# A graph layer with a mixture of experts: x multiplied before its norm, and the last experts' weights loaded elsewhere

## The chip, the cores and the metric

The kernel runs on one core of one Trainium2 chip. Its time is the device time of that core in microseconds, the median over several runs. TensorE is called PE below, VectorE DVE, ScalarE ACT, GpSimd POOL and SyncE SP; a DMA is issued from the instruction queue of SP, ACT or POOL.

## The reference

There are 3125 nodes with 256 features each, and 100000 edges sorted by their target. A layer norm of x (no gain or bias) feeds two branches: a graph convolution with a maximum over the edges of a target, and an attention-like mixer over all nodes. Their sum and x go through a second layer norm and a mixture of eight experts of which each node uses two:

```
xn = layernorm(x)
e = relu((xn[dst] - xn[src]) @ theta.T + theta_b + xn[src] @ phi.T + phi_b)
gnn = segment_max(e, dst)                   # 0 for a node with no edge
q, k, v = split(xn @ w_qkv.T)               # 8 heads of 64
dots = instance_norm(k).T @ instance_norm(v)
mix = (q @ dots / N) @ w_out.T + b_out
x = x + gnn + mix
xt = layernorm(x)
two experts by softmax(xt @ Wr + br), weights made to sum to 1
y_e = gelu(layernorm_e(xt) @ W1[e]) @ W2[e]  # 256 -> 1024 -> 256
x = x + sum of the two weighted y_e
```

## The kernel before

**Layout.** The nodes lie in 25 tiles of 128. `xnT(i)` holds the normalised tile i transposed (in the buffers `xn_lo` and `xn_hi`), `x_sb` the tile itself. The convolution is rewritten: since theta acts on the target and on the source, an edge's value is the target's `xn @ theta` plus the source's `b = xn @ (phi - theta)`, and the maximum has to be taken of the sources' `b` alone.

**Start.** While x loads, `search` (L258 to L287) finds the runs of edges in which nodes end, and POOL gathers 25 columns of keys (`run_keys`). `norm_stages` (L223), five steps skewed against each other over the tiles by `skewed`, takes mean and variance of a tile on DVE, the root on ACT, the reciprocal and `normalize` on DVE, transposes the normalised tile on PE into PSUM tile `tr`, copies it to `xnT`, multiplies by `wb = phi - theta` into PSUM tile `bp`, and copies that to `bt`. Every five tiles are stored to `b_d` in DRAM by one DMA on SP (L245 is the copy, `move` at L100 the store).

**Gathers and folds.** The edges lie in 782 steps of 128 edges, one per partition. POOL gathers the `b` rows of a step's sources (L107, 755 such gathers in the main loop), eight steps to a window in one of five buffers `wide` (named `g`), DVE folds each step into the running segment maximum (L366), and SP stores the windows to `s_d`. The steps are cut into four groups (`STEPS` = 240, 195, 194, 126), each of which finishes the nodes of its tiles (`GROUPS`: tiles 12 to 24, 5 to 11, 1 to 4, and 0).

**Behind a group.** When a group is folded, `group` (L1128) fetches the nodes' last rows from `s_d` (r gathers, POOL), `token_tile` (L422) adds the mixer's part (`without_edges`, L398, which multiplies `xnT` by theta and by the mixer's product into one PSUM tile `am` and adds x through an identity), norms the tile, and computes the router; `dispatch` (L1108) gives the rows to experts and scatters them to `xs_d` (L114). `Stream.go` (L720) is the experts' FFN of groups 0 to 2 on PE (L615 first product `hp`, L639 second product `yp`, L753 its bias), weights loaded expert by expert into three buffers `wts`. The mixer (`mixer`, L1008) runs beside the gathers of the first group.

**The last group.** Tile 0 has no scatter: `dense_tile` (L786) runs all eight experts over it in the order `DENSE` = 5, 6, 7, 0, 1, 2, 3, 4. The weights of 5, 6 and 7 are still in `wts`. Expert 0's first half is loaded into `xn_lo` during group 2's FFN, its second half into `xn_hi` when that FFN ends (L776, ACT queue); expert 1's two halves go into two `wide` buffers during the combines (L1323 to L1329, SP queue); 2, 3 and 4 (2 MB each) are loaded by `next_dense` (L1199, ACT queue) into `wts` as the first three experts are done. `scaled(k)` (L802) makes the input `xe` of phase k on DVE. Meanwhile `finale` gathers the FFN's rows `ys_d` back for every other tile (`combine`, 48 gathers), adds them (L1308) and stores them to `out` on SP. A combine chunk is four tiles, sometimes fewer, in a `wide` buffer: seven chunks follow one another.

**What sets the order.** The instruction order of PE, DVE, ACT and SP is written by the program itself. Tasks are Python generators; `start` puts one in a list and `tick` (L1063 to L1080) advances, after each gather of the main loop, every task that is due. What a task yields is the number of gather times (1.25 us) until it is due again. So a larger yield ahead of some instructions puts them later in their engines' queues, behind whatever other tasks emit meanwhile. POOL's own order is the order in which gathers and scatters are made. A transpose that stands early in PE's queue holds up everything behind it until its input is there; the maxima over nodes with no edge in tile 0 (`first_maxima`, L1207, transposes L1235) are such a place.

## Time and profile before

| what | us |
|---|---|
| median of 3 runs | 1219.15 (1218.51 to 1221.02) |
| profiled execution | 1217.85 |
| its span | 1216.0 |
| first gather of b_d rows | 48.19 |
| last gather of b_d rows | 1114.62 |
| last fold | 1120.05 |
| first matmul of the dense tile | 1140.36 |
| last store (`out<-o`) issued | 1208.98 |

All times inside the execution count from the start of its span. Busy time is what an engine spent in instructions; an instruction that waits for a semaphore shows as idle time before it, with the releaser in brackets, `[6.73 <-DMA b_d<-bt]` being 6.73 us idle, ended by a DMA. Where the releaser is called "issue", the profile shows no wait. By stretches: between 48 and 500 POOL is busy for 343.4 us and PE for 275.9 of 452; between 500 and 940 PE for 417.4 of 440; between 940 and 1006 PE for 24.1 of 66; between 1006 and 1120 PE for 106.3 of 114, with the DMA engines moving 357 GB/s; between 1120 and 1140.4 they move 97 GB/s; and in the last 75.6 us PE is busy for 61.4.

### The profile page before, as it was taken

To read this page: it belongs to the slowest core of one execution; us is meant where nothing else is said; L and a number is where in the kernel's file an instruction comes from. 1 tells how busy PE (TensorE), PEld (TensorE's weight loads), DVE (VectorE), ACT (ScalarE), POOL (GpSimd) and SP (SyncE) were. 2 spreads that over 40 slices of the span, in tenths; PEclk is the share of its full clock that TensorE was granted. 3 is DMA by queue.
4 is the path that set the end of the run, shared out by engine and by line. 5 is a ranking of instruction groups with operands and counts; after the bars stand their busy time and mean duration, and the time that the engine had idled before them with its cause. 6 is when DMAs were issued, how large, how long until landed. Compare 5 with 4: busy or idle time off the path is not lost.

```text
span 1216.0 us, 13364 instructions
## 1 busy us (share of the span) xinstructions
PE 938.2 (77%) x3929; PEld 670.4 (55%) x3929; DVE 678.6 (56%) x1998; ACT 326.0 (27%) x762; POOL 885.8 (73%) x911
## 2 busy tenths in 40 slices
PE   6556866645923548689999999979999527999986
PEld 5323433323311323258888887868887315777786
DVE  7669866685336772433333587455546764433633
ACT  4212222210101222133333343323332112332331
POOL 6677777777777777777777777777777777776733
PEclk9778888866965557889999999989999557999998
DMA  8668877666685664467888787689999658998683
GB/s 280 214 200 277 302 253 242 227 227 207 207 292 194 239 235 157 156 238 258 285 307 310 251 284 271 227 308 356 380 370 367 219 191 305 375 387 301 201 338 94
DMA packets 103928, 320.13 MB, mean 263 GB/s; under 512 B 20897, under 2 KB 44186, under 8 KB 92325
## 3 DMA queue, kind: packets, MB, share of 16 engines
q0 software_dynamic: 44032, 119.73, 31.5%
q1 hardware_dynamic: 29724, 115.08, 24.4%
q10 hardware_dynamic: 30089, 84.36, 19.3%
q8 instruction: 33, 0.54, 0.2%
q14 instruction: 50, 0.41, 0.1%
HBM read 192.05 MB, written 127.04 MB: 262 GB/s over the span
## 4 chain that ended last, share of the span: by engine, by line
PE 43%; DMA 5%; issue 4%; POOL 3%; DVE 2%; ACT 1%; ACTq 0%; POOLq 0%; DVEq 0%; SPq 0%
PE yp L639 18%; PE hp L615 18%; PE yp L753 3%; POOL g L107 2%; DMA w<-in_w 2%; DMA g<-b_d,srcI 2%; PE trf L698 1%; POOL xs_d L114 1%; DMA xn_lo<-b_d 1%; PE am L445 1%; DVE g L366 1%; PE mm L491 0%; DMA xn_hi<-xs_d 0%; DMA r<-s_d,end_i 0%; PE mm L403 0%
## 5 line engine op out<-in xcount | busy, mean ns | idle before, releaser
L107 POOL DMA_INDIRECT g<-b_d,srcI x755 | 738.2, 978 | 238.4 <-issue 203.8
L366 DVE SCALAR_TENSOR_TENSOR g<-g,cut 128x256 f32<-128x256 f32 x751 | 363.5, 484 | 356.8 <-DMA g<-b_d,srcI 339.0
L639 PE MATMUL yp<-w,hT 128*128 128x256 f32 (+1 forms) x1120 | 296.8, 387 | 0.0
L615 PE MATMUL hp<-xe,w 128*128 128x256 f32 (+2 forms) x1216 | 285.9, 361 | 11.5 <-issue 5.6
L615 PEld LDWEIGHTS hp<-xe,w 128*128 128x128 f32 x1216 | 216.7, 196 | 49.2 <-issue 18.0
L617 ACT ACTIVATE hT<-hp,sm 128x256 f32<-128x256 f32 (+2 forms) x320 | 140.2, 439 | 335.8 <-PE hp L615 335.3
L639 PEld LDWEIGHTS yp<-w,hT 128*128 128x128 f32 (+1 forms) x1120 | 201.1, 185 | 39.7 <-issue 12.4
L1012 PE MATMUL kv<-wkv,xn_lo 128*128 128x512 f32 x96 | 54.5, 720 | 38.0 <-DVE kn L1030 24.1
L1012 PE MATMUL kv<-wkv,xn_hi 128*128 128x512 f32 x104 | 59.3, 724 | 30.9 <-DVE kn L1030 30.2
L107 POOL DMA_INDIRECT g<-ys_d,from_i x48 | 46.1, 960 | 32.4 <-DVE g L1308 18.7
L445 PE MATMUL am<-cr,oh 128*128 128x257 f32 x86 | 37.3, 560 | 27.8 <-DVE r L450 19.9
L1012 PEld LDWEIGHTS kv<-wkv,xn_lo 128*128 128x128 f32 x96 | 21.1, 231 | 63.8 <-issue 60.3
L1012 PEld LDWEIGHTS kv<-wkv,xn_hi 128*128 128x128 f32 x104 | 22.8, 230 | 58.3 <-issue 55.6
L1228 DVE SCALAR_TENSOR_TENSOR xn_lo<-xn_lo,no_edge 128x256 f32<-128x256 f32 x96 | 45.9, 479 | 16.1 <-DMA xn_lo<-b_d 16.1
L401 PE MATMUL mm<-bias,ones 1*128 1x512 f32 x50 | 32.4, 731 | 16.2 <-ACT x_sb L408 12.9
L753 PE MATMUL yp<-b_sb,ident 8*128 8x256 f32 (+1 forms) x128 | 43.9, 422 | 0.0
L1016 ACT ACTIVATE sq<-kv 128x1024 f32<-128x1024 f32 x25 | 25.5, 1019 | 59.3 <-PE kv L1012 59.3
L445 PEld LDWEIGHTS am<-cr,oh 128*128 128x128 f32 x86 | 20.3, 267 | 37.1 <-issue 24.9
L709 ACT ACTIVATE xe<-trf,sm 128x256 f32<-128x256 f32 (+1 forms) x64 | 31.3, 544 | 27.6 <-PE trf L698 27.6
L1035 PEld LDWEIGHTS dots_p<-kn,vn 128*128 128x128 f32 x200 | 26.9, 199 | 19.0 <-issue 19.0
L1024 ACT ACTIVATE rsk<-var,eps 128x16 f32<-128x16 f32 x25 | 7.7, 308 | 110.7 <-DVE var L1021 110.7
L698 PE MATMUL trf<-ident,xn_hi 128*128 128x128 f32 (+1 forms) x128 | 19.2, 275 | 22.2 <-DMA xn_hi<-xs_d 22.2
(285 smaller groups left out, 991.1 us busy)
## 6 DMA issues: line engine op xcount, KB each, us to landing
s_d<-g SPq DMA_DIRECT2D x80, 1024.0 KB
w<-in_w ACTq DMA_DIRECT2D x84, 512.0 KB
w<-in_w ACTq DMA_DIRECT2D x6, 2048.0 KB
g<-b_d,srcI POOLq DMA_INDIRECT x755, 4.5
s_d<-g SPq DMA_DIRECT2D x13, 896.0 KB
xn_hi<-xs_d ACTq DMA_DIRECT2D x12, 512.0 KB
xs_d<-zero ACTq DMA_DIRECT2D x8, 512.0 KB
b_d<-bt SPq DMA_DIRECT2D x5, 640.0 KB
```

The costliest lines, as they stand in the source:

```text
L107: got = nc.gpsimd.indirect_dma_start(out=to, out_offset=None, in_=table, in_offset=row_index(index))
L366: nc.vector.scalar_tensor_tensor(g[:, j, :], last, cut[:, t:t + 1], g[:, j, :], op0=OP.add, op1=OP.max)
L401: nc.tensor.matmul(am, ones[0:1, :], bias, start=True, stop=False)
L445: nc.tensor.matmul(r2, picks[k], carried[g], start=(k == 0), stop=(k == len(slices) - 1))
L615: nc.tensor.matmul(hp[:, 0:n], w1t[:, c, f, :], xe[:, c, 0:n], start=(c == 0), stop=(c == 1))
L617: nc.scalar.activation(hT[f][:, 0:n], hp[:, 0:n], AF.Gelu, bias=sm[:, 4 + f, e:e + 1])
L639: nc.tensor.matmul(yp[r][0:part, :], hT[q][:, r * part:(r + 1) * part], w2t[:, q, :], start=(q == 0), stop=(q == FC - 1 and self.whole))
L698: nc.tensor.transpose(tr[:, c, r * n:(r + 1) * n], self.held["xs", u // 2][0:n, u % 2 * 2 + r, c * P:(c + 1) * P], ident[0:n, 0:n])
L709: nc.scalar.activation(xe[:, c, 0:n], self.held["tr", u][:, c, 0:n], AF.Identity, bias=sm[:, 2 + c, e:e + 1], scale=sm[:, c, e:e + 1])
L753: nc.tensor.matmul(yp[0:n, :], ident[0:E, e:e + 1].to_broadcast([E, n]), b2_sb, start=False, stop=True)
L1012: nc.tensor.matmul(kv[:, k, :], xnT(i, c), wkv[:, c, k * INNER:(k + 1) * INNER], start=(c == 0), stop=(c == 1))
L1228: nc.vector.scalar_tensor_tensor(of_k[:, k, :], b, no_edge[:, k, i:i + 1], of_k[:, k, :], op0=OP.add, op1=OP.max)
```

## The change

Five things are done.

1. The first norm is no longer applied to x before the transposes. x itself is transposed (`of_x`) and multiplied (`of_sources`); the weights (`wb`, theta in `am_w`, the mixer's `wkv` and `wq`) are centred over their input dimension (`centred`: a matmul with ones and one DVE operation), so that the mean of x drops out, and the products are scaled by the tile's reciprocal deviation `rs_x` when they leave PSUM. Deviations are taken for five tiles at a time (`deviations`). The transposes run `lead` = 7 tiles ahead of the products; the stores to `b_d` are cut by `STORES`, the last of them having two tiles. The keys' gathers are started before `wb` is made. `without_edges` brings the bias and x in through a diagonal of the deviations.
2. Steps around the first lot of group 2's FFN are put closer together (`soon`).
3. Expert 1's two halves and expert 0's second half are loaded by `more_weights`, started after the last fold, on SP's queue, each into a buffer that a one-column memset claims first. The dense tile's first input is made when the FFN's last lot begins ("last lot").
4. The scatters of groups 0 and 1 come five gathers later (yield 14 in place of 9).
5. A yield of 8 stands before the transposes of `first_maxima`.

Parts of the diff that only rename or allocate, and the variant for other graphs at the end of the file, are left out.

```diff
--- before.py
+++ after.py
@@ -48,6 +48,7 @@
 REST = T - COL[G]
+STORES = (0, 5, 10, 15, 20, 23, NT)
 W = 8
@@ -220,31 +223,43 @@
-    def norm_stages(work, ps, i, wb=None, b_rows=None, held=None):
-
-        mean, var = moments(work, x_sb[:, i, :], 0)
-        rs = work.tile([P, 1], F32, name="rs")
-        nc.scalar.activation(rs, var, AF.Sqrt, bias=eps)
-        yield
-        nc.vector.reciprocal(rs, rs)
-        xn = work.tile([P, D], F32, name="xn")
-        normalize(xn, x_sb[:, i, :], mean, rs)
+    def of_x(work, ps, i):
+
+        st = work.tile([P, nc.vector.BN_STATS_DIM], F32, name="st0")
+        nc.vector.bn_stats(st, x_sb[:, i, :])
+        mv = work.tile([P, nc.vector.BN_AGGR_DIM], F32, name="mv0")
+        nc.vector.bn_aggr(mv, st)
+        nc.vector.tensor_copy(std[:, i:i + 1], mv[:, 1:2])
         tr = ps.tile([P, 2, P], F32, name="tr")
         for c in range(2):
-            nc.tensor.transpose(tr[:, c, :], xn[:, c * P:(c + 1) * P], ident)
+            nc.tensor.transpose(tr[:, c, :], x_sb[:, i, c * P:(c + 1) * P], ident)
         yield
         nc.scalar.copy(xnT(i), tr)
+
+    def deviations(i0, i1):
+        nc.scalar.activation(std[:, i0:i1], std[:, i0:i1], AF.Sqrt, bias=eps)
         yield
-        if wb is not None:
-            bp = ps.tile([P, D], F32, name="bp")
-            for c in range(2):
-                nc.tensor.matmul(bp, xnT(i, c), wb[:, c, :], start=(c == 0), stop=(c == 1))
-            yield
-            if i % 5 == 0:
-                held["bt"] = work.tile([P, 5, D], F32, name="bt", bufs=2)
-            nc.scalar.copy(held["bt"][:, i % 5, :], bp)
-            if i % 5 == 4:
-                move(nc.sync, b_rows[:, i - 4:i + 1, :], held["bt"])
+        nc.vector.reciprocal(rs_x[:, i0:i1], std[:, i0:i1])
+
+    def of_sources(work, ps, i, wb, b_rows, held):
+
+        bp = ps.tile([P, D], F32, name="bp")
+        for c in range(2):
+            nc.tensor.matmul(bp, xnT(i, c), wb[:, c, :], start=(c == 0), stop=(c == 1))
+        yield
+        i0 = max(k for k in STORES if k <= i)
+        if i == i0:
+            held["bt"] = work.tile([P, 5, D], F32, name="bt", bufs=2)
+        nc.scalar.activation(held["bt"][:, i - i0, :], bp, AF.Copy, scale=rs_x[:, i:i + 1])
+        if i + 1 in STORES:
+            move(nc.sync, b_rows[:, i0:i + 1, :], held["bt"][:, 0:i + 1 - i0, :])
+
+    def centred(w, p):
+
+        for c in range(2):
+            nc.tensor.matmul(p, ones, w[:, c, :], start=(c == 0), stop=(c == 1))
+        nc.vector.scalar_tensor_tensor(w, p[:, None, :].to_broadcast([P, 2, p.shape[-1]]), -1.0 / D, w, op0=OP.mult,
+                                       op1=OP.add)
@@ -395,17 +410,20 @@
+    diag = keep.tile([P, 2, P], F32, name="diag")
+
     def without_edges(ps, i):
+        nc.scalar.activation(diag[:, i % 2, :], ident, AF.Copy, scale=std[:, i:i + 1])
         am = ps.tile([P, 2 * D], F32, name="mm")
-        nc.tensor.matmul(am, ones[0:1, :], bias, start=True, stop=False)
+        nc.tensor.matmul(am, diag[:, i % 2, :], bias, start=True, stop=False)
         for c in range(2):
             nc.tensor.matmul(am, xnT(i, c), am_w[:, c, :], start=False, stop=False)
-        nc.tensor.matmul(am[:, D:2 * D], ident, x_sb[:, i, :], start=False, stop=True)
+        nc.tensor.matmul(am[:, D:2 * D], diag[:, i % 2, :], x_sb[:, i, :], start=False, stop=True)
         on_pe(3.1)
         yield 3
-        nc.scalar.copy(xn2(i), am[:, 0:D])
-        nc.scalar.copy(x_sb[:, i, :], am[:, D:2 * D])
+        for to, k in ((xn2(i), 0), (x_sb[:, i, :], 1)):
+            nc.scalar.activation(to, am[:, k * D:(k + 1) * D], AF.Copy, scale=rs_x[:, i:i + 1])
@@ -736,12 +754,13 @@
                 if ("xe", u) not in self.held:
+                    soon = self.lots[u][0] == G - 2
                     self.rows(u // 2)
-                    yield 8
+                    yield 3 if soon else 8
                     self.turn(u)
-                    yield 2
+                    yield 1 if soon else 2
                     self.scaled(u)
-                    yield 2
+                    yield 1 if soon else 2
                 g, e, h = self.lots[u]
@@ -768,12 +787,13 @@
                 w1t, w2t = self.held["w", q]
+                if u + 1 == len(self.lots) and not self.open:
+                    clock["last lot"] = True
                 for _ in units.run(e, w1t, self.held["xe", u], w2t, done, between, 2, self.half(u)):
...
                 dense_w[DENSE[k]] = self.held["w", q - 2 + k]
-            dense_half(0, 1, xn_hi[:, 0:FC, :].rearrange("p i d -> p (i d)"), nc.scalar)
             clock["through"] = True
@@ -802,9 +821,13 @@
+        if ready is not None:
+            while "last lot" not in ready:
+                yield 1
+        scaled(0)
+        yield 1
         while ready is not None and "through" not in ready:
             yield 1
-        scaled(0)
         o = act.tile([P, D], F32, name="o", bufs=1)
@@ -862,18 +885,45 @@
     move(nc.scalar, wb, phiT.rearrange("(c p) o -> p c o", p=P))
+    am_b = once.tile([1, 3 * D], F32, name="am_b")
+    move(nc.scalar, am_b[:, 0:D], bout)
+    move(nc.scalar, am_b[:, D:3 * D], gbias)
     run, keys, run_keys = search(ea, once, ps0, dst)
     load_x()
+    run_keys()
     nc.vector.tensor_sub(wb, wb, am_w[:, :, 0:D])
...
-    run_keys()
     b_rows = b_d.rearrange("(i p) d -> p i d", p=P)
     b_held = {}
-    skewed((norm_stages(work, ps1, i, wb, b_rows, b_held) for i in range(NT)), ((4, 5), (3, 4), (2, 3), (1, 2), (0, 0)))
+    tiles = [of_x(work, ps1, i) for i in range(NT)]
+    by_five = [deviations(i, i + 5) for i in range(0, NT, 5)]
+    sources = [of_sources(work, ps1, i, wb, b_rows, b_held) for i in range(NT)]
+    lead = 7
+    for k in range(NT + lead + 1):
+        if 0 <= k - lead - 1:
+            next(sources[k - lead - 1], None)
+        if 0 <= k - 1 < NT:
+            next(tiles[k - 1], None)
+        if k < NT:
+            next(tiles[k], None)
+        for ago in (1, 0):
+            if 0 <= k - ago < NT and (k - ago) % 5 == 4:
+                next(by_five[(k - ago) // 5], None)
+        if k == 2:
+            centred(wb, ps1.tile([P, D], F32, name="bp"))
+        if 0 <= k - lead < NT:
+            next(sources[k - lead], None)
+    nc.vector.tensor_add(am_b[:, D:2 * D], am_b[:, D:2 * D], am_b[:, 2 * D:3 * D])
+    bias_p = ps1.tile([P, 2 * D], F32, name="tr")
+    for k in range(2):
+        nc.tensor.matmul(bias_p[:, k * D:(k + 1) * D], ones[0:1, :], am_b[:, (1 - k) * D:(2 - k) * D],
+                         start=True, stop=True)
+    centred(am_w[:, :, 0:D], ps1.tile([P, D], F32, name="bp"))
+    nc.scalar.copy(bias, bias_p)
     first.close()
@@ -902,11 +950,14 @@
         yield 20
-        nc.vector.tensor_add(bias[:, 0:D], am_b[:, D:2 * D], am_b[:, 2 * D:3 * D])
-        nc.vector.tensor_copy(bias[:, D:2 * D], am_b[:, 0:D])
         move(nc.scalar, wq_sb, wq.rearrange("(r p) d -> p r d", p=P))
         move(nc.scalar, wo_sb, woT.rearrange("(r p) o -> p r o", p=P))
-        yield 10
+        yield 8
+        for r in range(4):
+            nc.vector.tensor_reduce(wq_m[:, r:r + 1], wq_sb[:, r, :], AX.X, OP.add)
+        nc.vector.tensor_scalar(wq_m, wq_m, 1.0 / D, None, op0=OP.mult)
+        yield 2
+        nc.vector.tensor_tensor(wq_sb, wq_sb, wq_m[:, :, None].to_broadcast([P, 4, D]), OP.subtract)
         move(nc.scalar, s_d[0:1, :], low)
@@ -1004,6 +1055,9 @@
         nc.vector.tensor_tensor(wkv_h, wkv_h, wm[:, :, None].to_broadcast([P, 4 * HEADS, DH]), OP.subtract)
+        kv = p2.tile([P, 2, INNER], F32, name="kv")
+        for k in range(2):
+            centred(wkv[:, :, k * INNER:(k + 1) * INNER], kv[:, k, :])
@@ -1013,9 +1067,10 @@
         sq = mixp.tile([P, 2 * HEADS, DH], F32, name="sq")
-        nc.scalar.activation(sq, kv.rearrange("p k (h e) -> p (k h) e", e=DH), AF.Square)
+        nc.scalar.activation(sq, kv.rearrange("p k (h e) -> p (k h) e", e=DH), AF.Square,
+                             scale=rs_x[:, i:i + 1])
         vn = mixp.tile([P, INNER], F32, name="vn")
-        nc.scalar.copy(vn, kv[:, 1, :])
+        nc.scalar.activation(vn, kv[:, 1, :], AF.Copy, scale=rs_x[:, i:i + 1])
         yield 3
@@ -1025,7 +1080,8 @@
         both = mixp.tile([P, HEADS], F32, name="both")
-        nc.vector.tensor_mul(both, rs[:, 0:HEADS], rs[:, HEADS:2 * HEADS])
+        nc.vector.scalar_tensor_tensor(both, rs[:, 0:HEADS], rs_x[:, i:i + 1], rs[:, HEADS:2 * HEADS], op0=OP.mult,
+                                       op1=OP.mult)
         kn = mixp.tile([P, HEADS, DH], F32, name="kn")
@@ -1117,7 +1173,7 @@
         yield from slots(ro, mm, g, half, i0, i1, made[0], taken)
-        yield 1 if g == G - 2 else 9
+        yield 1 if g == G - 2 else 14
         put = []
@@ -1229,6 +1285,7 @@
         most = at_hand["first"].tile([P, 2, FIRST], F32, name="most")
+        yield 8
         for c in range(2):
@@ -1320,13 +1377,6 @@
             yield 2 * nt
-            if g == 0 and i == i0 + W // 2:
-
-                while "shared" not in clock:
-                    yield 1
-                yield 6
-                for k in range(2):
-                    dense_half(1, k, wide.tile([P, HALF], F32, name="g"))
         if i1 == NT:
@@ -1337,6 +1387,19 @@
             yield from combines(g)
+
+    def more_weights():
+
+
+        for k in range(2):
+            to = wide.tile([P, HALF], F32, name="g")
+            nc.vector.memset(to[:, 0:1], 0.0)
+            dense_half(1, k, to)
+        while "last lot" not in clock:
+            yield 1
+        to = xn_hi[:, 0:FC, :].rearrange("p i d -> p (i d)")
+        nc.vector.memset(to[:, 0:1], 0.0)
+        dense_half(0, 1, to)
@@ -1362,6 +1425,8 @@
             clock["last"] = last
+            if g == G - 1:
+                start(more_weights(), clock["now"] + 1)
             if g == 0:
```

## The prediction

> **What bounds the kernel now.** I read four views in this order: the page's busy shares with the groups of line L107, the list of waits on POOL, the chain that ended last, and the timeline at the places where the chain changes engine.
>
> ```profile
> PE 938.2 (77%) x3929; PEld 670.4 (55%) x3929; DVE 678.6 (56%) x1998; ACT 326.0 (27%) x762; POOL 885.8 (73%) x911
> L107 POOL DMA_INDIRECT g<-b_d,srcI x755 | 738.2, 978 | 238.4 <-issue 203.8
> ...
> POOL g L107 <- issue: 216.0, 703, 2.1
> POOL g L107 <- DVE g L1308: 18.7, 3, 10.8
> POOL g L107 <- DMA b_d<-bt: 6.7, 1, 6.7
> ```
>
> Nearly all of the idle time before the 755 gathers is "issue": 0.3 us between two of them, no wait for data. One wait for data is long, 6.7 us, and it is before the first gather. So POOL is a metronome (0.978 + 0.30 us a gather) that begins when b_d is stored, and everything up to the last gather slides with that moment. The timeline there:
>
> ```profile
> 41.80 1.89 PE L241 MATMUL bp<-wb,xn_hi 128*128 128x256 f32 x8
> 43.73 0.37 ACT L245 COPY bt<-bp 128x256 f32<-128x256 f32 x1 [0.49 <-PE bp L241]
> 44.12 0.36 SPq L100 DMA_DIRECT2D b_d<-bt  x1
> 48.19 0.94 POOL L107 DMA_INDIRECT g<-b_d,srcI  x1 [6.73 <-DMA b_d<-bt]
> ```
>
> The last product ends near 43.6, the copy follows, the store is issued at 44.12, and the gather starts 4.6 us after the last product. The 6.73 also tell how long POOL was free before: its key gathers were done by 41.5.
>
> Group 2's FFN holds PE from 1006 to 1140, and its stretch shows one hole of size:
>
> ```profile
> 1018.41 1.03 PE L639 MATMUL yp<-w,hT 128*88 128x256 f32 x4
> 1021.10 0.33 PE L1235 MATMUL mm<-ident,xn_lo 128*128 128x128 f32 x1 [1.66 <-DVE xn_lo L1228]
> 1021.91 0.47 PE L1235 MATMUL mm<-ident,xn_lo 128*128 128x128 f32 x1 [0.48 <-DVE xn_lo L1228]
> 1023.33 0.47 PE L1235 MATMUL mm<-ident,xn_lo 128*128 128x128 f32 x1 [0.95 <-DVE xn_lo L1228]
> 1024.82 0.48 PE L1235 MATMUL mm<-ident,xn_lo 128*128 128x128 f32 x1 [1.02 <-DVE xn_lo L1228]
> 1025.09 1.38 PE L615 MATMUL hp<-xe,w 128*128 128x176 f32 x4
> ```
>
> These are transposes put into PE's order before their DVE maxima were ready. After the last fold (1120) the token path of tile 0 runs to the first dense matmul at 1140.36, called D below; then come eight expert phases of about 7.0 us, counted here from 0. The second hole is before phase 6:
>
> ```profile
> 1165.72 0.94 POOL L107 DMA_INDIRECT g<-ys_d,from_i  x1 [10.80 <-DVE g L1308]
> 1182.22 0.94 POOL L107 DMA_INDIRECT g<-ys_d,from_i  x1 [6.81 <-DVE g L1308]
> ...
> 1186.15 0.48 DVE L1308 SCALAR_TENSOR_TENSOR g<-g,share,x_sb 128x256 f32<-128x256 f32 x1 [3.57 <-DMA g<-ys_d,from_i]
> 1187.08 0.60 DVE L802 TENSOR_SCALAR xe<-xT,sm 128x128 f32<-128x128 f32 x2
> ...
> 1187.52 1.19 PE L615 MATMUL hp<-xe,w 128*128 128x128 f32 x4 [5.59 <-issue]
> ```
>
> Read from below: PE waited 5.59 us for xe (L802); xe stood in DVE's order behind a combine operation (L1308) that waited for a gather of ys rows; that gather was issued at 1182.22 because its buffer was still being read by the store to out issued at 1164.66, whose last packets landed at 1181.45, while a 2 MB expert load was in flight. The weights themselves were in time: the three expert loads landed at 1164.9, 1172.9 and 1180.4, for phases that begin at 1175, 1187 and 1198.
>
> **The change, part by part.** The sum is made against the profiled execution, 1217.85 (span 1216.0). The median of the runs is 1219.15, 1.3 above; I forecast between the two bases. About 0.2%, 2.4 us, is what a measurement of this kernel can tell from no change.
>
> *Start.* Removed on DVE: 25 normalise operations (0.55) and 20 of 25 reciprocals (0.13); on ACT 20 of 25 square roots (0.30). Added: five square roots and reciprocals for five tiles each, a 128x1 copy per tile, the centring of wb (two matmuls, one DVE operation of 128x512, like L867's 0.63), and a scale in the eviction that was a copy anyway (0.37, no longer). PE's matmuls stay: per tile two transposes and two 256-wide products (two records each in the timeline, x4 a tile's products). What the change buys is order: the transposes no longer wait for normalised x, so PE runs ahead by seven tiles. Working: from the timeline, per tile, transposes take about 0.66 and products 1.47 before 18.7, and 0.36 and 0.73 after it. Changed PE order: transposes 0 to 2, centring, transposes 3 to 7, product 0, and then alternately. From 9.5: 3 x 0.66 + 1.5 + 5 x 0.66 = 6.8, plus 1.1 for the wait for centred wb: product 0 at 17.4. Left then: 17 x 0.36 + 25 x 0.73 = 24.4, so the last product ends at 41.8, or 42.5 if the fast pace begins at 18.7 as now. Before: 43.6. The last store shrinks from five tiles (640 KB, 44.12 to 47.41 = 3.29 us) to two (256 KB); the trace has 128 KB (out<-o) in 2.0 and 640 KB in 3.29, so 2.4: 0.9 gained. Gain 2.0 to 2.7; I take 2.3. Bounds: the key gathers (moved before the subtraction, 0.45 earlier) still end near 41.0, so POOL's wait can shrink by at most 6.9; on the small side 0.5, if the slow pace lasts to 21.5. Below nothing is excluded only if the second table load stays short: Sqrt now comes after copies, so ACT has one load more, for which the timeline's row is 1.28 us (1.76 to 3.04); ACT has some 0.2 us idle per tile (1.06 of 1.25 used, 0.3 less afterwards) to take it in.
>
> [...] Row first: the granted clock reads 1.00 in every 2 us window from 6 to 22, yet four product matmuls take 1.91 until 17.4 and 1.03 from 19.1. [...]
>
> *Scatters of groups 0 and 1 five gathers later*: 5 x 1.25 = 6.3 us later for their FFN lots. Group 1's lots end by 940 and group 2's begin at 1006; in that stretch PE is busy 24.1 of 66.0 us. That gap hides the whole delay; without it 6.3 us would be paid. On POOL only the place of the scatters changes, not their number. Centring of wkv, am_w and wq, the diag operations (25 on ACT), moved loads and the scaled mixer evictions: POOL is the bound in 48 to 500 (PE busy 275.9 of 452), so nothing.
>
> *First lots of group 2 ("soon")*: PE waits for a DMA of scattered rows there, so nothing.
>
> *Eight gathers' time before the maxima's transposes*: the hole of 1.66 + 0.48 + 0.95 + 1.02 = 4.1 us and the slow matmuls after it (about 1.8) go, 5.9 in all, on PE. But PE's order behind it also changes: of the 11 us of FFN matmuls that now fill gaps of the token path (1125 to 1140) 8.9 stand before the first token matmul (L1287, now 1122.36). That becomes 1122.4 + 8.9 - 5.9 = 1125.3, and from L1287 to the dense start (18.0 now) I count 14.6, since in the timeline some 3.4 us of token steps stand ready behind an FFN group: D = 1139.9, against 1140.4. What is late next is the token path itself. Lower bound -3.5 (waits for w, 0.51 and 1.99 with slow matmuls behind, go as well), upper +4 (they grow: the DMA queues move 357 GB/s in 1006 to 1120). I take 0.
>
> *Weights behind the last fold*: three 1 MB loads move from 1141 to 1147 (landed 1149.2, 1155.1, 1158.5) to about 1121 to 1123, into a stretch where the queues move 97 GB/s (1120 to 1140). At the pace of the trace (1 MB in 8 to 11 us, two or three at once) they land before D. Each has a memset of 128x1 before it on DVE (0.15 by the 128x1 rows). Queued behind them on SP is the store of combine results only; r gathers may share the engines with them (landed 1124.9, needed 1126.8, so 1.9 spare). On their own they hid nothing: phase 4 and 5 began on time. What they free is 1146 to 1158 for the out stores and the first 2 MB load.
>
> *Tail order*: in the changed DVE order xe of phase 6 stands behind all six gathers of the sixth combine chunk (before: its first tile), xe of phase 7 behind all eight of the seventh. With s the start of the sixth chunk's gathers (before D + 41.9), xe 6 comes at s + 10.7 (5 x 1.25 issue, 3.9 to the DVE operation, its own pair 0.5), xe 7 ten us later, and the end at s + 31.9 after D. Before: D + 68.6 to the end of the last matmul's eviction. So nothing changes at s = D + 36.7. s is bound by the fifth chunk's gathers: 8 x 1.25 after a start of D + 23.7 (before 25.4, released by the out store that ran behind the moved weights), so 33.7; and by the third chunk's store, which may straggle behind the 2 MB loads as now, 41.9. I take 34.7, since the stretch that delayed these stores is cleared: -2. Ends -8 (the hole and its slow matmuls gone, 5.6 + 2.4) and +5.3.
>
> *Sum*: -2.3 + 0 - 2 = -4.3. From 1217.85: 1213.6; from the median: 1214.9. Forecast 1214.3.
>
> **Rivals.**
> - *The tail hole closes entirely.* Without 2 MB in its way the third chunk's store lands at once, s falls below D + 30, the tail gives 8: 1218.5 - 2.3 - 8 = 1208. For it: the last expert loads alone moved 16 KB packets at over 400 GB/s, so gaps open between them. Against: they still run, and xe now stands behind more gathers.
> - *The start's gain is eaten* (cold pace, table load, waits for centred wb) and the tail stays: 0.5 off, 1218. The forecast that the change does nothing measurable. [...]
> - *Slower: DVE's head of the line.* If the third chunk's store straggles as now, s stays at D + 41.9 and both xe wait for whole chunks: +5.3, less 2.3 at the start: 1218.5 + 3 = 1221.5. It decides from s later than about D + 39. For it: the store was issued during one 2 MB load and ended with the next, and those loads keep their times. Against: the stores before it get out sooner.
>
> **How the numbers follow.** Forecast 0.47 (its own range 1210.5 to 1217.5: faster 0.43, same 0.04); hole closed 0.17 (faster); start eaten 0.13 (same 0.12, slower 0.01); head of the line 0.23 (same 0.06, slower 0.17). Faster 0.60, same 0.22, slower 0.18. The range 1207 to 1222 leaves out the outer parts of the second and fourth case and mishaps with w.
>
> **What would show it.** Right: first g gather near 45.9 instead of 48.19; no L1235 waits; the last am L1287 near 1123 (1125.3 less 2.3) with D 2 us earlier than before; the 1 MB loads landed before D; the sixth chunk's first gather at most 36 us after D. Wrong: product matmuls still at 1.9 for four after 20; PE waits for w<-in_w grown beyond 3 us in 1006 to 1120; a PE idle of over 6 us before phase 6 or 7 with L802 behind L1308.

## The result, and the profile after

The change made the kernel slower. Over 16 runs of each on the same chips the median is 1226.24 us against 1220.09, ratio 1.0041 (95% interval 1.0022 to 1.0059), some 5 us (the ratio is not that of the two medians, which lie 6.2 us apart). The profiled execution of the changed kernel took 1223.48 us (span 1221.6). Both profiled executions lay under their medians (1217.85 by 2.2, this one by 2.8), so the two profiles differ by about what was measured; single stretches of them have to be taken with care: a second profile of the kernel before, e4 below, differs from the first by up to 5.8 us.

The start first; the lines are from the timeline of the changed kernel (start, duration, engine, line, operation, what the idle time before it waited for), the one without an engine from its critical chain (start, time from issue to landing).

```profile
12.08 1.78 PE L235 MATMUL tr<-ident,x_sb 128*128 128x128 f32 x6
...
15.68 1.03 PE L248 MATMUL bp<-wb,xn_lo 128*128 128x256 f32 x4
...
42.06 0.84 ACT L253 ACTIVATE bt<-bp,rs_x 128x256 f32<-128x256 f32 x2 [2.09 <-DMA b_d<-bt]
...
42.92 3.58 DMA b_d<-bt
...
47.41 0.94 POOL L108 DMA_INDIRECT g<-b_d,srcI  x1 [6.38 <-issue]
```

The products begin at 15.7, earlier than I had put them, and at the quick pace from the first (1.03 us for four). But the last two tiles then wait 2.09 us for one of the two `bt` buffers, whose store is on its way, and the last store, issued at 42.92, lands at 46.50: 3.58 us for two tiles, where five tiles took 3.29. The first gather comes at 47.41 in place of 48.19. Of 2.3 us there are 0.8.

The list of waits on POOL (idle us in total, times, longest) and the costliest group of the page:

```profile
POOL g L108 <- issue: 220.6, 698, 6.4
...
POOL g L108 <- DMA out<-g: 12.3, 1, 12.3
...
POOL r L108 <- DVE g L381: 4.7, 7, 2.9
...
POOL r L108 <- DMA s_d<-g: 2.9, 2, 1.8
```

```profile
L108 POOL DMA_INDIRECT g<-b_d,srcI x755 | 745.3, 987 | 238.5 <-issue 208.4
```

The 755 gathers are busy for 745.3 us against 738.2, 9 ns more each; beyond 0.95 us each that is 28.0 us against 21.0. The last of them begins at 1121.25, against 1114.62: POOL lost 7.4 us between its first gather and its last, a stretch that the prediction took for fixed, and in this profile 7.0 of them are these longer gathers. Then the token path is shorter, as forecast in kind (the first dense matmul 23.0 us after the last gather, before 25.7), and the tail is not:

```profile
1157.32 0.42 DVE L844 TENSOR_TENSOR x_sb<-x_sb,mm 128x256 f32<-128x256 f32 x1 [2.10 <-PE mm L843]
1157.66 0.48 DVE L1365 SCALAR_TENSOR_TENSOR g<-g,share,x_sb 128x256 f32<-128x256 f32 x1
...
1178.01 0.49 DVE L1365 SCALAR_TENSOR_TENSOR g<-g,share,x_sb 128x256 f32<-128x256 f32 x1 [8.88 <-DMA g<-ys_d,from_i]
...
1185.32 0.59 DVE L821 TENSOR_SCALAR xe<-xT,sm 128x128 f32<-128x128 f32 x2
```

```profile
1171.79 0.94 POOL L108 DMA_INDIRECT g<-ys_d,from_i  x1 [12.31 <-DMA out<-g]
```

```profile
1185.76 1.19 PE L633 MATMUL hp<-xe,w 128*128 128x128 f32 x4 [5.44 <-issue]
```

In DVE's new order the second combine chunk's sums (L1365) stand behind the second bias (L844), which waits for PE. Its store to `out` is issued 17.5 us after the first dense matmul (before: 12.9), and the fifth chunk's gathers, which wait for that store, start at 27.5 us, before 25.4. PE's hole is about as large as before (5.44 for 5.59 us) and only one phase earlier. From the first dense matmul to the end it takes 77.3 us, before 75.6.

### The profile page after: what moved, and what is told of

Its sections match the earlier page's. It is cut to its first block, busy times and chain, and to the rows that moved or that the text cites. A ratio compares the mean times of both kernels' runs of the same rounds, so it can differ in the third digit from the quotient of the medians.

```text
span 1221.6 us, 13395 instructions
## 1 busy us (share of the span) xinstructions
PE 934.1 (76%) x3949; PEld 675.3 (55%) x3949; DVE 676.4 (55%) x1990; ACT 343.6 (28%) x769; POOL 894.5 (73%) x911
## 4 chain that ended last, share of the span: by engine, by line
PE 48%; DMA 18%; POOL 14%; DVE 10%; issue 8%; ACT 1%; POOLq 0%; SPq 0%; DVEq 0%; ACTq 0%
PE hp L633 18%; PE yp L657 18%; POOL g L108 11%; DMA g<-b_d,srcI 10%; DVE g L381 3%; DMA w<-in_w 3%; PE yp L772 3%; PE kv L1066 2%; POOL xs_d L115 2%; PE bp L248 1%; DMA r<-s_d,end_i 1%; PE trf L716 1%; DMA xs_d<-xn_hi,slot_i 1%; DMA s_d<-g 1%; PE am L463 1%
## 5 line engine op out<-in xcount | busy, mean ns | idle before, releaser
L108 POOL DMA_INDIRECT g<-b_d,srcI x755 | 745.3, 987 | 238.5 <-issue 208.4
L657 PE MATMUL yp<-w,hT 128*128 128x256 f32 (+1 forms) x1120 | 292.7, 383 | 0.0
L657 PEld LDWEIGHTS yp<-w,hT 128*128 128x128 f32 (+1 forms) x1120 | 199.0, 183 | 39.1 <-issue 11.6
L1066 PE MATMUL kv<-wkv,xn_lo 128*128 128x512 f32 x96 | 56.2, 740 | 23.5 <-DVE kn L1086 23.5
L419 PE MATMUL mm<-bias,diag 128*128 128x512 f32 x50 | 31.6, 717 | 43.8 <-ACT diag L417 39.3
L1284 DVE SCALAR_TENSOR_TENSOR xn_lo<-xn_lo,no_edge 128x256 f32<-128x256 f32 x96 | 45.9, 479 | 26.3 <-DMA xn_lo<-b_d 26.3
L1066 PEld LDWEIGHTS kv<-wkv,xn_lo 128*128 128x128 f32 x96 | 22.0, 239 | 50.5 <-issue 47.3
L1070 ACT ACTIVATE sq<-kv,rs_x 128x1024 f32<-128x1024 f32 x25 | 27.8, 1112 | 65.0 <-PE kv L1066 65.0
L463 PEld LDWEIGHTS am<-cr,oh 128*128 128x128 f32 x86 | 19.9, 262 | 38.1 <-issue 23.8
L419 PEld LDWEIGHTS mm<-bias,diag 128*128 128x128 f32 x50 | 8.4, 206 | 52.2 <-ACT diag L417 46.8
```

Of the source, the lines that this page charges most:

```text
L108: got = nc.gpsimd.indirect_dma_start(out=to, out_offset=None, in_=table, in_offset=row_index(index))
L419: nc.tensor.matmul(am, diag[:, i % 2, :], bias, start=True, stop=False)
L463: nc.tensor.matmul(r2, picks[k], carried[g], start=(k == 0), stop=(k == len(slices) - 1))
L657: nc.tensor.matmul(yp[r][0:part, :], hT[q][:, r * part:(r + 1) * part], w2t[:, q, :], start=(q == 0), stop=(q == FC - 1 and self.whole))
L1066: nc.tensor.matmul(kv[:, k, :], xnT(i, c), wkv[:, c, k * INNER:(k + 1) * INNER], start=(c == 0), stop=(c == 1))
L1070: nc.scalar.activation(sq, kv.rearrange("p k (h e) -> p (k h) e", e=DH), AF.Square, scale=rs_x[:, i:i + 1])
```

## The experiments

Each run has one profile. The table, worked out from starts in the timelines, cuts it at the same places: A is the first gather of b_d rows; B, C and D are what gathers 1 to 250, 250 to 600 and 600 to 755 took beyond 1.25 us each (C and D hold the other gathers and the scatters between them); E is the last gather; F from there to the first dense matmul; G from that to the end. W is what POOL waited, beyond its usual 0.3 us, at three places: the two lots of scatters of group 1 (part of C) and the first r gather of group 2 (part of D). It will be needed below.

| kernel | parts | A | B | C | D | E | F | G | W | ratio of times |
|---|---|---|---|---|---|---|---|---|---|---|
| before | none | 48.2 | 11.6 | 92.4 | 19.9 | 1114.6 | 25.7 | 75.6 | 2.7 | 1 |
| e4 | none | 48.2 | 12.7 | 95.3 | 21.7 | 1120.4 | 23.7 | 77.0 | 5.5 | |
| e3 | 3 | 48.2 | 13.2 | 92.6 | 21.7 | 1118.2 | 26.5 | 80.6 | 1.9 | 1.0034 |
| e2 | 2 to 5 | 48.2 | 14.2 | 88.1 | 23.1 | 1116.1 | 23.4 | 79.9 | 2.3 | 0.9994 |
| e1 | 1 | 47.9 | 12.1 | 101.2 | 21.3 | 1125.0 | 22.1 | 77.2 | 12.6 | 1.0046 |
| e10 | 1, 4 | 47.2 | 16.6 | 90.8 | 28.1 | 1125.2 | 25.0 | 81.9 | 9.3 | 1.0046 |
| after | all | 47.4 | 16.7 | 92.4 | 22.3 | 1121.3 | 23.0 | 77.3 | 1.5 | 1.0041 |
| e9 | all | 47.3 | 17.0 | 89.8 | 29.3 | 1125.9 | 24.7 | 76.8 | 7.7 | 1.0041 |
| e11 | all but 3 | 47.2 | 14.6 | 89.6 | 26.3 | 1120.3 | 25.7 | 76.2 | 7.5 | 1.0010 |
| e12 | all, third bt | 47.6 | 13.9 | 90.1 | 25.9 | 1120.1 | 24.2 | 76.6 | 7.1 | 1.0044 |
| f1 | all, diagonals moved | 46.9 | 16.5 | 91.7 | 26.0 | 1123.6 | 22.3 | 77.1 | 8.2 | 1.0070 |
| f2 | all, maxima held | 46.9 | 16.5 | 90.4 | 23.8 | 1120.2 | 21.8 | 76.6 | 3.3 | 1.0031 |
| f3 | all but 3, both edits | 47.2 | 16.1 | 89.5 | 22.8 | 1118.1 | 21.6 | 77.4 | 3.3 | 0.9987 |

**The halves.** e1 is the kernel before with part 1 of the change alone, e2 with parts 2 to 5, e3 with part 3 (and the dense tile's first input at the last lot), e4 the kernel before itself.

> The kernel before with part 1 of the change alone (x transposed raw, centred weights, keys earlier, stores cut by STORES). Theory A (the gather stretch is longer by 7.4 us in the one profile of the changed kernel by chance): ratio 0.999, gathers 0.8 us earlier throughout, tail as before. Theory B (part 1 shifts the phase of the folds on DVE against the gathers on POOL, so that more gathers take over 1.02 us): ratio 1.003 to 1.005, last gather of b_d rows 4 to 7 us later than in the kernel before, over 180 gathers longer than 1.02 us. Theory C (the later scatters do it): as A here.

> The kernel before with parts 2 to 5 and without part 1. Theory A: ratio 0.999, since the token path gains 2.7 and the tail loses 1.7. Theory B: 0.998 to 1.000, first gather and gather stretch as before. Theory C: ratio 1.003 to 1.005, with the last gather 4 to 7 us later. In all three the fifth combine chunk's first gather comes 27 us after the first dense matmul and a PE wait of over 5 us stands before phase 5, not phase 6.

> The kernel before with part 3 alone (expert 1's halves and expert 0's second half loaded behind the last fold, and the dense tile's first input made at the last lot). If the tail is worse because the second combine chunk's sums now stand behind the second bias in DVE's order: time from the first dense matmul to the end 77 us against 75.6, ratio 1.001; if the loads of 3 MB in the token path cost anything, the first dense matmul comes more than 26 us after the last gather (25.7 before).

> The kernel before, unchanged, profiled once more: how far the gather stretch varies by itself. By chance alone (theory A): last gather anywhere from 1111 to 1122. If the stretch is a property of the program (B, C): within 2 us of 1114.6, and 100 to 130 gathers over 1.02 us.

Measured: e1 1.0046 (1.0015 to 1.0076), e2 0.9994 (0.9966 to 1.0022), e3 1.0034 (1.0004 to 1.0065). e4's last gather came at 1120.4, 5.8 us later than in the first profile of the same program: the stretch isn't fixed, as theory A said. But e1 is slower by as much as the whole change, which theory A denied, and not in the way of theory B: 115 long gathers, not 180. Theory C fails by e2, which has the later scatters and lost nothing. In e1 POOL has a new long wait:

```profile
753.80 1.18 POOL L115 DMA_INDIRECT xs_d<-xn_lo,slot_i  x1 [9.14 <-ACT hT L635]
```

POOL waits 8.8 us beyond its usual 0.3 at the first scatter of group 1, and 3.7 at the second (before: 1.5 and 0.9; e4: 1.5 and 3.4, so only the first of the two stands out). What it needs there are the slots that the token steps of group 1 work out (`slot_i`, on DVE at 752.84; before, 746.20); the releaser in the brackets, an ACT operation of the FFN, is only what came last by the profile. The cause lies 250 us earlier. On PE, in the kernel before and in e1:

```profile
497.40 1.12 PE L401 MATMUL mm<-bias,ones 1*128 1x512 f32 x2
...
500.79 1.12 PE L401 MATMUL mm<-bias,ones 1*128 1x512 f32 x2
...
520.24 2.07 PE L401 MATMUL mm<-bias,ones 1*128 1x512 f32 x2 [12.58 <-ACT x_sb L408]
...
528.09 2.02 PE L615 MATMUL hp<-xe,w 128*128 128x256 f32 x8 [0.66 <-ACT xe L709]
```

```profile
497.47 1.12 PE L419 MATMUL mm<-bias,diag 128*128 128x512 f32 x2 [1.22 <-ACT diag L417]
...
501.96 1.13 PE L419 MATMUL mm<-bias,diag 128*128 128x512 f32 x2 [1.22 <-ACT diag L417]
...
520.77 2.08 PE L419 MATMUL mm<-bias,diag 128*128 128x512 f32 x2 [15.53 <-ACT diag L417]
...
525.75 1.02 PE L419 MATMUL mm<-bias,diag 128*128 128x512 f32 x2
...
530.20 1.13 PE L419 MATMUL mm<-bias,diag 128*128 128x512 f32 x2 [1.28 <-ACT x_sb L426]
...
534.86 2.02 PE L633 MATMUL hp<-xe,w 128*128 128x256 f32 x8 [0.95 <-ACT xe L727]
```

A tile of `without_edges` takes 4.49 us there in place of 3.39, since each waits for its diagonal, which stands in ACT's order behind the evictions of the tile ahead. But PE is idle for 15.53 us soon after, so these 1.1 us a tile are not by themselves what is lost. What counts is the place of the last diagonals. ACT, in e1:

```profile
519.93 0.33 ACTq L101 DMA_DIRECT2D xn_hi<-xs_d  x1
520.31 0.69 ACT L417 ACTIVATE diag<-ident,std 128x128 f32<-128x128 f32 x2 [14.20 <-issue]
```

The load of the scattered rows, `xn_hi<-xs_d`, is issued from ACT's queue and only when the scatters are done (5.3 to 5.7 us after the last of them began, in all thirteen profiles of the table). The diagonals behind it wait with it. In the kernel before, one tile of `without_edges` is left on PE then (at 520.24, waiting for an eviction behind the same load); in e1 three are (520.77, 525.75, 530.20), and the FFN's first transposes stand behind them. The thirteen profiles order themselves by this count:

| tiles left when the load is issued | profiles | from the load's issue to the first matmul of the FFN, us |
|---|---|---|
| 0 | e2 | 5.3 |
| 1 | before, e3, e4 | 8.9 to 9.2 |
| 2 | after, e9 to e12, f1 to f3 | 10.7 to 11.4 |
| 3 | e1 | 14.9 |

So part 1 leaves two more tiles behind the load, with part 4's later scatters or without, and costs the FFN some 6 us of its start: counted from the second lot of scatters (499.3 in e1, 498.4 before) it begins 35.6 us after in e1 and 29.6 before, 30.9 to 31.7 after with parts 1 and 4 and 25.5 in e2. Nothing makes that up: from its first matmul to the end of group 1's lots the FFN takes 409 to 416 us in all thirteen profiles, whenever it begins. The token steps of group 1, which share PE's order with it, come later too (their slots' first matmul at 745.66, before 738.98), so POOL stands at the scatter.

Up to the last fold e3 is the old program. Behind it DVE's timeline shows what happens with three loads of 1 MB issued at that place:

```profile
1130.61 0.42 DVE L439 TENSOR_TENSOR r<-r,kept 128x256 f32<-128x256 f32 x1 [2.92 <-DMA r<-s_d,end_i]
```

The r gather, issued at 1124.5, lands at 1130.5, 6.0 us later; before, 1120.0 to 1122.8. The prediction gave it 1.9 us to spare and no price. F is 26.5, and G is 80.6, not the 77 expected: the second combine chunk's store is issued 12.6 us after the first dense matmul, as before, so the reason named did not occur. PE has a second hole there, 2.87 us at 60.4 (e2, with G 79.9, has 2.78 at 61.2); where these come from was not followed.

**Another chip.** Four runs went to a chip on which the kernel before takes 1767 us and the changed kernel's DMA moves 184 GB/s in place of 261. There e5 (the changed kernel) has the ratio 0.9939 (0.9896 to 0.9981), e6 (parts 1 and 4) 0.9957 (0.9907 to 1.0006), e7 (without part 3) 0.9897 (0.9804 to 0.9989), e8 (a third `bt` buffer and the diagonals moved) 0.9818 (0.9704 to 0.9931).

> The changed kernel once more. In its first profile the stretch from the first to the last gather of b_d rows is 1073.8 us, and its 755 gathers take 28.0 us more than 0.95 us each; two profiles of the kernel before have 1066.4 and 1072.2 us, and 21.0 and 23.2. If that is chance: stretch 1066 to 1072 and 21 to 25 here, and the time comes from elsewhere. If it is a property of the changed program: 1073 or more and 27 or more.

> Part 1 with part 4 (scatters of groups 0 and 1 five gathers later). Part 1 alone (ratio 1.0046) showed POOL waiting 8.8 and 3.7 us at the scatters of group 1, behind an FFN that began 6.8 us later. If that wait is part 1's cost, part 4 takes it away: waits under 2 us, last gather of b_d rows at 1114 to 1119 against 1125, ratio 1.000 (0.998 to 1.002). If part 1 costs its time elsewhere, the ratio stays at 1.004.

> The changed kernel without part 3: expert 1's halves and expert 0's second half loaded where the kernel before loads them. Part 3 alone measured 1.0034, with the r gather landing 6.0 us after its issue against 2.7, and a tail of 80.6 us against 75.6. If it costs the same in the company of the other parts: ratio 1.000 to 1.001, r landing in under 3.5 us, tail 75 to 77 us. If the other order on PE hides it: ratio 1.004 as for the changed kernel.

> The changed kernel with three buffers bt in place of two, and each diagonal of group 0's tiles made before the evictions of the tile ahead of it. If the last store to b_d waits for a buffer (2.1 us on ACT at 42.06 in the changed kernel), the first gather comes at 45.3 us against 47.4; if the diagonal is what PE waits for (1.2 us a tile from 495 to 505), those waits go and group 0's FFN starts 3 to 5 us earlier against the second scatter. Time: 2 us under the changed kernel, ratio 1.002; if the gather stretch decides, no difference from it (1.004).

None of this could be read against the theories: POOL's longest waits there are for stores of the folded windows, a bound that the other chips don't have (the longest such wait there is 8.0 us, in e9). From e5's list:

```profile
POOL g L108 <- DMA s_d<-g: 216.0, 20, 41.0
```

**The same four again, on a chip at the usual pace.**

> The changed kernel on a chip at the usual pace (the four runs before were on a chip on which the kernel before took 1767 us). If its long gather stretch (1073.8 us, 28.0 us over 0.95 us a gather) is chance: stretch 1066 to 1072 and 21 to 25. If it is a property of the changed program: 1073 or more and 27 or more.

> Part 1 with part 4. If the scatter wait (8.8 and 3.7 us in part 1 alone) is what part 1 costs: waits under 2 us, last gather of b_d rows at 1114 to 1119 against 1125, ratio 1.000 (0.998 to 1.002). If part 1 costs its time elsewhere: 1.004.

> The changed kernel without part 3. If part 3 costs in the company of the others what it costs alone (1.0034): ratio 1.000 to 1.001, r landing within 3.5 us of its issue, tail 75 to 77 us. If the other order on PE hides it: 1.004.

> The changed kernel with three buffers bt, and each diagonal of group 0's tiles made before the evictions of the tile ahead. If the last store to b_d waits for a buffer: first gather at 45.3 us against 47.4. If PE waits for the diagonal: the 1.2 us waits from 495 to 505 go and group 0's FFN starts 3 to 5 us earlier after the second scatter. Ratio 1.002; if the gather stretch decides, 1.004.

The edit of e10 is part 1 and `yield 1 if g == G - 2 else 14`; of e12

```diff
-            held["bt"] = work.tile([P, 5, D], F32, name="bt", bufs=2)
+            held["bt"] = work.tile([P, 5, D], F32, name="bt", bufs=3)
...
+        if GROUPS[0][0] <= i < GROUPS[0][1] - 1:
+            make_diag(i + 1)
```

Measured: e9 1.0041 (1.0008 to 1.0074), e10 1.0046 (1.0015 to 1.0076), e11 1.0010 (0.9976 to 1.0044), e12 1.0044 (1.0012 to 1.0076). e10: the scatter waits went as expected (0.9 and 0.9 us), C fell from 101.2 (e1) to 90.8, and the time did not move. A new wait has taken their place; from e9, where it stands as well:

```profile
960.27 1.12 POOL L108 DMA_INDIRECT r<-s_d,end_i  x1 [7.96 <-DMA s_d<-g]
```

It is group 2's first r gather, which needs the stored fold windows. In e9, e10, e11 and e12 POOL stands there for 7.7, 7.5, 6.9 and 5.8 us beyond its usual 0.3; in the kernel before for 0.3, in e4 0.6, in e2 2.2, in the first profile of the changed kernel 1.5. (That profile's POOL reaches the place at 956.2, the others with parts 1 and 4 at 949.7 to 954.3; its gathers had been longer.) Just ahead of it on DVE and SP, in e9:

```profile
942.14 0.48 DVE L1284 SCALAR_TENSOR_TENSOR xn_lo<-xn_lo,no_edge 128x256 f32<-128x256 f32 x1 [7.14 <-DMA xn_lo<-b_d]
...
950.22 0.48 DVE L1284 SCALAR_TENSOR_TENSOR xn_lo<-xn_lo,no_edge 128x256 f32<-128x256 f32 x1 [3.77 <-DMA xn_lo<-b_d]
```

```profile
951.12 3.21 SPq L101 DMA_DIRECT2D s_d<-g  x2
```

The folds stand in DVE's order behind the maxima (L1284), those wait for their loads of b_d tiles, and the window's store is issued late. Group 1's FFN, whose last weight load is issued at 942.4 in e9 and at 930.4 in the kernel before, ends at 951.6 and 939.5. In e12 the wait for `bt` is gone from the timeline. But its products, which begin at 15.7 as in e9, ran at the slow pace at first (1.91 us for four, until 20.7) and end 1.7 us later, at 42.9; the first gather is at 47.6, so the run doesn't say what the third buffer is worth. The diagonals there still hold PE 1.2 us a tile and leave two tiles behind the load.

**Three more on the wait and its cause.** f1 puts group 0's diagonals in two tiles of their own, made one tile ahead. f2 holds the maxima back:

```diff
-            while "tokens" in clock and "routed" not in clock:
+            while (i >= 18 or "tokens" in clock) and "routed" not in clock:
                 yield 1
```

f3 has both edits and leaves part 3 out.

> The changed kernel with group 0's diagonals in two tiles of their own, each made one tile ahead of its use. Theory K: the diagonals hold PE up 1.2 us a tile, so group 0's FFN begins 31 us after the second half's scatter (25.5 in the kernel with parts 2 to 5 alone), group 1's FFN ends later, its weight loads fall on the loads that the folds stand behind, and POOL waits 5.8 to 7.7 us at group 2's first r gather. Then here: FFN 26 to 28 us after the scatter, the wait at the r gather 2 to 4 us, ratio 1.001 to 1.003. Rival: the diagonals run beside PE's idle time, FFN start and wait unchanged, ratio 1.004.

> The changed kernel with the maxima over tiles 18 to 24 (xn_lo loads on SP and their DVE operations) held back until group 2's tokens are routed, so that nothing of them lies between the folds and the stores from 915 to 960. If those loads are what delays the folds, the store and so POOL: the wait at group 2's first r gather is under 1 us, the last gather of b_d rows comes 5 to 7 us earlier than in the changed kernel's second profile (1125.9), ratio 0.998 to 1.001. If the wait comes from the FFN's weight loads alone: wait and ratio unchanged (6 to 8 us, 1.004). The dense tile may start later, if the maxima are now late.

> Both edits together, and part 3 undone (expert 1's halves and expert 0's second half loaded where the kernel before loads them). If the wait at the r gather and part 3 are what the change costs, nothing of the loss is left: ratio 0.996 to 0.999. If the longer gathers (over 0.95 us each, 21 to 28 us in all) belong to part 1: 1.001 to 1.003.

f1: 1.0070 (1.0035 to 1.0105), wait 4.8 us. The edit didn't do what it was for (PE still waits 1.22 us a tile for the diagonal, the FFN begins 30.9 us after the scatter): a diagonal made one tile ahead still stands behind the load in ACT's order, and two tiles are left there as without the edit. So it says nothing on either theory, and its larger ratio is not explained. f2: 1.0031 (1.0000 to 1.0062), the wait at the r gather 2.7 us, the last gather 5.7 us earlier than in e9 and 2.5 earlier than the mean of the six profiles with parts 1 and 4 and without the edit: the trace goes the way of the theory, more weakly than "under 1", and the ratio can't be told from 1.0041. As the changed kernel's first profile had 1.5 us without the edit, that the maxima pass the FFN's delay on to POOL is made likely by this, not shown. f3: 0.9987 (0.9959 to 1.0016), wait 1.5 us: the loss is gone, without any gain that can be told from none. Since f3 differs from the changed kernel in part 3 as well, it doesn't say how much of the loss went with the wait.

**Parts 2, 4 and 5 by themselves** (g1), part 5 alone (g2), and g1 with f2's edit (g3) were to tell whether what is left of the change is a gain.

> The kernel before with parts 2, 4 and 5 alone (soon, later scatters, the yield before the maxima's transposes). If the parts add up (all parts 1.0041; without part 3 1.0010; without part 1 0.9994; part 1 alone 1.0046; part 3 alone 1.0034), these three give what is left, 0.996 to 0.997. If part 4 and 5 only help what part 1 and 3 disturb: 0.999 to 1.001.

> The kernel before with part 5 alone. The stall of 4.1 us and the slow matmuls after it (5.9 in all) go from PE between 1019 and 1027. If the FFN of group 2 sets the end: first dense matmul up to 5 us earlier against the last scatter of group 2 (139 us in the kernel before), ratio 0.996. If the token path of tile 0 does: matmuls of the FFN stand before the token steps instead, the distance unchanged within 1 us, ratio 0.999 to 1.001.

> Parts 2, 4 and 5 with the maxima over tiles 18 to 24 held back until group 2's tokens are routed. With parts 1 to 5 this edit took the wait at group 2's first r gather from 6 to 8 us to 2.7. With parts 2 to 5 that wait is 2.2 us; here it falls under 1, so 1 to 2 us less than the run without it: 0.995 to 0.998.

They too ran on a chip, not the one of e5 to e8, on which the kernel before takes 1766 us: 0.974 (0.967 to 0.981), 1.006 (1.002 to 1.010) and 0.993 (0.989 to 0.997). Of the three g1 is the best there, and part 5 alone gains nothing. On the usual chips g1 wasn't run, and whether it beats the kernel before there stays open.

**What adds up.** On the usual chips the ratios fit a sum: part 1 some +0.46% (e1, and e10 with part 4), part 3 +0.3% (e3; all parts against e11), the other three together about -0.4% (e2 less e3), which gives +0.4% for all, as measured, and +0.1% for e11. Each term has an uncertainty of about 0.3% and the last of 0.4%, so this is a sum that fits, not one that is shown; f1's 1.0070 lies 0.3% above it.

In the table, the six profiles with parts 1 and 4 and the maxima not held back (e9 to e12, after, f1) against the three whose gather stretch is the old program (before, e4, e3): A -0.9, B +3.4, C -2.7, D +5.2 on the mean, together +5.0 at the last gather. With all parts (after, e9, e12, f1) F is 23.5 on the mean and G 77.0, against 24.7 and 76.3 in before and e4. C and D can be read further. Without the waits of W, C is 88 to 92 and D 19 to 22 in all thirteen profiles: what moves them is the waiting. W is 1.9 to 5.5 us in the four profiles without part 1 (3.1 on the mean), 1.5 to 12.6 in the seven with it and the maxima not held back (7.7), and 3.3 in f2 and in f3. That is 4.6 us of some 5. Part 4 does not take the waiting away, it moves it from C to D. A profile shows either kind of loss: in the first one of the changed kernel W is only 1.5, and its 7.4 us are longer gathers.

B is less certain. Parts 2 to 5 change nothing before the scatters of group 0 near 460, so up to there all nine kernels with part 1 run the same work (but for e12's third `bt`), and their B goes from 12.1 to 17.0 (15.6 on the mean) against 11.6 to 14.2 (12.9) in the four without it. Most of it is in longer gathers.

## Why the prediction was wrong

- *The step that failed* is the first reading: "POOL is a metronome (0.978 + 0.30 us a gather) that begins when b_d is stored, and everything up to the last gather slides with that moment." From it followed "POOL is the bound in 48 to 500 [...], so nothing" for the diagonals and the mixer, and "That gap hides the whole delay" for the scatters. That POOL showed no waits only meant that everything it needs was in time. The diagonals, costed at nothing, stood in ACT's order behind the load of the scattered rows, left two more tiles to do there, and so put the start of the FFN some 6 us back. The FFN had no slack to make that up: the table on record had PE busy for 417.4 of the 440 us between 500 and 940, where PE, not POOL, sets the pace. POOL then waited for what came late, 8.8 and 3.7 us at the scatters of group 1 in e1, and, when part 4 had moved these, 4.8 to 7.7 us at group 2's first r gather in five of six profiles. I had looked for cover in PE's idle 940 to 1006 and not asked what POOL needs from DVE and SP in that stretch. The way from the late FFN to the scatters can be followed line by line; the way to the r gather, over the maxima and their loads, is likely (W is 3.3 in f2 and f3, which hold the maxima back) and not shown.
- *B, +3.4 us in the mixer's stage on the mean of those six* (+2.6 over all nine with part 1), wasn't forecast at all. The two groups overlap (11.6 to 14.2 without part 1, 12.1 to 17.0 with it), and the runs don't say which of part 1's operations makes the gathers longer, if one does; that stays open.
- *Start*: gain 0.3 to 1.3 in the nine profiles with part 1, 0.9 on the mean, for 2.3. The products were earlier than costed: in six of the nine the last one ends at 41.2 (costed 41.8, before 43.7). The term that failed is the last store, 2.4 us estimated. Issued between 42.9 and 44.9, it lands between 46.0 and 47.0, and hardly sooner when it is issued sooner (3.58 us in the profile above, 2.1 in e1, where it was issued 1.9 us later). The wait for `bt` buffers I had not looked for, but as the landing doesn't follow the issue, its price isn't shown. In e1, e12 and f3 the slow pace did last, to 19.6 to 20.7, as the rival "the start's gain is eaten" had it; the last product ends at 42.9 to 43.1 there.
- *The maxima's transposes and the token path*: right, and more profiles show it better than one. The L1235 waits are gone. With parts 2 and 5 the path from the first token matmul to the dense tile takes 15.0 to 15.2 us (eight profiles; 14.6 forecast), without them 18.0 to 18.2, and 20.9 in e3. The first token matmul stands 121.3 to 124.9 us after the last scatter (122.8 on the mean) against 118.1 to 121.3 (120.1), 2.7 later for the 2.9 forecast. So the two nearly cancel, as the sum had it.
- *Weights behind the last fold*: costed at nothing with 1.9 us to spare. The reading behind that was wrong: the r gather landed at 1122.75, not 1124.9 (at 1124.95 PE begins a transpose), so 4.0 us were to spare. In e3, where part 3 is alone, it landed 3.3 us later after its issue, and the kernel took 1.0034 (1.0004 to 1.0065). Whether part 3 costs anything in company isn't shown: e11 without it is 1.0010 and e9 with it 1.0041 on one chip, but the intervals overlap, and F and G of the two differ by 1.0 and 0.6 us in opposite directions.
- *Tail*: -2 forecast, +0.7 measured on the mean, where the two profiles of the kernel before themselves have 75.6 and 77.0. What failed is that nothing was gained. The term was the start of the fifth chunk's gathers, D + 23.7 forecast, 27.5 measured, and with it the sixth chunk's, 37.5 for 34.7. In the new order the second chunk's sums stand behind the second bias: their store is issued 17.0 to 17.5 us after the first dense matmul in all eight profiles with parts 2 and 5, 12.6 to 12.9 in the five without. What that costs isn't shown, as e4, with the old order and its store at 12.9, starts the fifth chunk at 27.1 too. The rival "DVE's head of the line" had named the mechanism, for a later chunk; by its own point of decision, D + 39, it should have cost nothing, and no cost can be told.

The sum with the measured terms: start -0.9, gathers +5.9, token path -1.2, tail +0.7, so +4.5, against 5.0 (2.7 to 7.2) measured. That it comes so near is in part luck, since single profiles of one kernel differ by as much as 5.8 us.

## What to carry to other kernels

An engine that shows no waits isn't thereby independent (POOL's wait at the first scatter of group 1 is 1.5 us in the kernel before and 8.8 in e1): ask, for each kind of instruction on it, how late its inputs could come before it would wait, and follow that back through the order of every queue on the way, SP's stores included. A small operation added ahead of each of many tiles is costed on the engine that waits for it, not on the one that runs it, and by what stands ahead of it in its own queue: here a load that waits for something else (in e1 PE was idle for 15.53 us before the diagonal behind it came). And two profiles of the same program should be laid side by side before a stretch is called fixed: here its length differs by 6 us.

## What the runs showed of the hardware

- **Gathers that begin just behind a fold take longer.** In the first profile of the kernel before, 85 gathers began 0.1 to 0.3 us after a fold on DVE began; they took 1.10 us on the mean, 76 of them over 1.02. The other 670 took 0.96, 32 of them over 1.02. In the second profile it is 104 gathers at 1.11, in the two of the changed kernel 114 and 102 at 1.10. Such a pair, from the changed kernel's timeline, behind an undisturbed one:

```profile
207.21 0.48 DVE L381 SCALAR_TENSOR_TENSOR g<-g,cut 128x256 f32<-128x256 f32 x1 [0.83 <-DMA g<-b_d,srcI]
...
208.19 0.95 POOL L108 DMA_INDIRECT g<-b_d,srcI  x1 [0.30 <-issue]
...
210.54 0.48 DVE L381 SCALAR_TENSOR_TENSOR g<-g,cut 128x256 f32<-128x256 f32 x1 [2.85 <-DMA g<-b_d,srcI]
...
210.69 1.16 POOL L108 DMA_INDIRECT g<-b_d,srcI  x1 [0.30 <-issue]
```

  The excess over 0.95 us is 21 to 28 us in a run, and a fold's moment depends on when its gather landed, which may be a part of why the time of one program varies as it does (1211 to 1233 us for the kernel before on one chip; of the 5.8 us between its two profiles 2.2 are longer gathers). What makes them longer isn't shown: no run took the folds away from the gathers.
- **The same start ran at two paces.** In the first profile of the changed kernel the first product matmuls, at 15.7, take 1.03 us for four; ahead of them PE had run eight tiles of transposes and four centring matmuls since 8.8, with waits of up to 1.3 us. Six of the nine profiles with this start are like it. In e1, e12 and f3 four products take up to 1.9 us until 19.6, 20.7 and 19.7, and the granted clock reads 0.50, 0.59 and 0.50 between 16 and 18; in the six it reads 1.00. The wait just ahead of the products doesn't tell them apart: 1.5 us in e9 and f2 as in e12. Why three of the nine ran at the lower clock, no run shows. The 1.00 that I read for the kernel before from 6 to 22 says little: the first record of a granted clock in that trace begins at 18.4, with the quick pace.
- **A store's landing did not follow its issue.** Two tiles (256 KB), with another store and the last key gathers still landing ahead of them, took 3.58 us when issued at 42.92 and 2.1 when issued at 44.86 or 44.17 (e1, f3); in the nine profiles they landed between 46.0 and 47.0. Five tiles (640 KB) took 3.3 in the four profiles without part 1.
- **Chips differ.** The same kernel before took 1220 to 1222 us on three of them and 1766 and 1767 on two, and the sign of the change differs with it (1.0041 on the usual ones, 0.9939 on one of the others).
